# A decoder layer with a mixture of experts: order of fetches, routing steps and sends where attention ends

## The chip, the core and the metric

The kernel runs on one core of a Trainium2 chip. The metric is the device time of one launch in microseconds. Before the change three runs took 1261.08 us (median), from 1258.22 to 1261.12.

The engines are named as in the profile: PE (TensorE, matrix products and transposes), PEld (its weight loads), DVE (VectorE), ACT (ScalarE), POOL (GpSimd) and SP (SyncE, here only an issuer of DMAs).

## What is computed

A pre-norm decoder layer on 32 sequences of 112 tokens and 256 channels, all in float32: windowed causal self-attention, cross-attention to 375 context rows with a relative bias, and a feed-forward part in which each token goes to the two best of eight experts. Cut to the feed-forward part, which the change touches most:

```
x = x + self_attention(layernorm(x))
x = x + cross_attention(layernorm(x), ctx, rel_bias)

xf = layernorm(x).reshape(3584, 256)
probs = softmax(xf @ router_w.T)                       # 8 experts
topv, topi = top_k(probs, 2)
probs = probs * mask(topi)
probs = probs / (probs.sum(-1) + 1e-9)
h = silu(xf @ gate_w[e] + gate_b[e]) * (xf @ up_w[e] + up_b[e])   # 512 wide, per expert e
y = sum_e probs[:, e] * (h_e @ down_w[e] + down_b[e])
x = x + y
```

## The kernel before

**Groups and slots.** The 32 sequences form eight groups `g` of four. Attention is a software pipeline of numbered slots: each slot holds one item of scores, softmax and average of some group, and a table (`steps`, `late`) says which other steps are issued in which slot. `base[g]` is the first cross-attention slot of group g; a group takes 16 slots, and `base[NG]` (NG = 8) is the first slot after the last scores. PE, DVE and ACT run their instructions exactly in the order in which the slots issue them (`manual_schedule`), and POOL is held to the order of issue too (`pool_order`), apart from pairs of DMAs that are marked loose. So where a step stands in the table is where it stands in each engine's queue.

**Routing a group** (`put_route`). After its last norm (`norm`, `scale`, `norm_t`), a group's tokens go through seven steps, one slot each: `choose` (logits to exp), `rank` (softmax, then all comparisons of the eight probabilities), `front` (ties), `gate` (which two experts), `weight_gates` (the two weights), `count` (positions behind the tokens counted so far, in `taken`) and `address` (row numbers). Nearly every step is a DVE instruction, then a POOL one, then a DVE one. Then `send` scatters the group's normed rows into a DRAM buffer `xslots` in which each expert has its region: eight indirect DMAs from POOL, two for each of the four sequences. `turn_gates` and `down_bias` add the gate-weighted down bias to the residual `x`, and SP writes it to the output.

**Experts.** 39 tiles of 256 or 128 rows are worked off in the list `order`. For tile k, POOL issues an indirect fetch of the expert's weights (`fetch_weights`, 128 x 3080 floats, 1.58 MB) and one or two of its rows out of `xslots` (`fetch_rows`, 128 x 265 floats each). PE transposes the rows (`turned_in`, DVE copies them to `xT`), multiplies by gate and up weights (`hidden`, four steps f of eight matmul instructions; ACT `sil`, DVE `hid`), then by the down weights (`down`); ACT scales `y` and POOL scatters it into the output with an add. Tiles run one behind: `down` of tile k-1 comes after `hidden` of tile k. The first ten tiles are planned once six groups are counted, the rest after the last group (`later_plan`).

**The seam.** Tile 0's `hidden` steps are placed in the last attention slots (`begin`, `go_on`); `experts()` starts in slot `base[NG] + 5`, fetches tile 2 at once and tile k+3 when tile k starts. At this place the last group (g = 7) still has its norm and its whole routing ahead, and group 6 its sends: both are interleaved with the first expert tiles. PSUM tiles of kind `pj` (two buffers) are used by averages, `ops`, `count`, `gtp`, `dbps` and `py`, those of kind `sc` (four buffers) by scores and `gu`, those of kind `tr` (two) by transposes.

Lines that the prediction steps through: `fetch_weights` L949, `fetch_rows` L962, `send` L725, `turned_in` L1004 and L1008, `hidden` L1018 to L1026, `down` L1037 to L1044, `attended` L597 and L602, `divide` and `turn` L568 to L584, `count` L698 to L706, `rank` L641 to L651, `weight_gates` L676 to L688, `turn_gates` L749, `down_bias` L762 and L767, the last norm's POOL part L349 to L352 and its ACT part L363.

Of the kernel before, what the change touches and what calls it, by code (L numbers as in the profile page):

```python
# [11 lines left out]
F32 = mybir.dt.float32  # L12
# [7 lines left out]
B, S, D = 32, 112, 256  # L20
H, DH = 16, 16
K = 375
# [3 lines left out]
P = 128  # L26
GB = 4
NG = B // GB
# [50 lines left out]
def decoder_kernel(  # L79
# [95 lines left out]
    with ExitStack() as att, ExitStack() as own_att:  # L175
# [179 lines left out]
        def scale(g, n, b2):  # L355
            if b2 == 0:
                tag, width = ("xr", ROW) if n == 3 else ("xn", D)
                pool = keep if n == 3 else selfp
                xn = pool.tile([S, GB, width], F32, tag=tag, name=f"xn{g}_{n}")
                normed[g, n] = xn, *normed[g, n]  # L360
            xn, rstd, shift = normed[g, n]
            for b in (2 * b2, 2 * b2 + 1):
                nc.scalar.activation(  # L363
                    xn[:, b, :D], xs[g][:, b, :], AF.Identity,
                    bias=shift[:, b:b + 1], scale=rstd[:, b:b + 1],
                )
            if b2 == 1:
                normed[g, n] = [xn]
# [54 lines left out]
            )  # L423

        def cross_queries(g, c):
            if c == 0:
                cross_q[g] = two.tile([P, NC2, 2, GT], F32, tag="q_cross", name=f"q_cross{g}")
            ps = ps_pj.tile([P, GT], F32, tag="pj", name=f"q2ps{g}_{c}")
            project(ps, wq_sb[:, :, c * P:(c + 1) * P], normed[g, 2][1])
            by_parity(cross_q[g][:, c], ps, g == 0)  # L430

        def load_context(g, b):
            ct = two.tile([P, NC2, K], F32, tag="ct", name=f"ct{g}_{b}")
# [30 lines left out]
        def scores(cross, selfs):  # L464

            name = "_".join(str(v) for part in (cross or (), *selfs) for v in part)
            w = two.tile([S, 4, K + S], F32, tag="w", name=f"w{name}", bufs=3)
            low = small.tile([S, 3, 4], F32, tag="low", name=f"low{name}")
            at = K if cross else 0
            sc = [ps_sc.tile([S, 512], F32, tag="sc", name=f"sc{name}_{r}") for r in range(4)]  # L470
            if cross:
                g, b, s = cross
                c, p = divmod(s, 2)
                kT, q = keys[g, b][1], cross_q[g]
                for r in range(4):
                    rows = slice(32 * r, 32 * r + 32)
                    scored[cross] = nc.tensor.matmul(  # L477
                        sc[r][:, :K], q[rows, c, p, b * S:(b + 1) * S], kT[rows, c, :],
                        start=True, stop=True,
                    ).ins  # L480
            if selfs:
                g, b, s = selfs[0]
                c, p = divmod(s, 2)
                n, at_b = len(selfs), slice(b * S, (b + 1) * S)
                q, k = self_in[g, c]
                for r in range(4):
                    rows = slice(32 * r, 32 * r + 32)
                    nc.tensor.matmul(  # L488
                        sc[r][:, at:at + n * S].rearrange("q (p k) -> q p k", p=n),
                        q[rows, at_b], k[rows, p:p + n, at_b], start=True, stop=True,  # L490
                    )
            spans = []
            if cross:
                spans.append((0, K))
            spans += [(at + i * S, at + (i + 1) * S) for i in range(len(selfs))]
            for r in range(4):
                for i, (lo, hi) in enumerate(spans):
                    if cross and i == 0:
                        c, p = divmod(cross[2], 2)
                        add = bias[:, 8 * c + 2 * r + p, :]  # L500
                    else:
                        add = wmask
                    nc.vector.tensor_tensor_reduce(  # L503
                        out=w[:, r, lo:hi], in0=sc[r][:, lo:hi], in1=add,
                        scale=-1.0, scalar=FAR, op0=ALU.add, op1=ALU.min,
                        accum_out=low[:, i, r:r + 1],
                    )
            for i, (lo, hi) in enumerate(spans):
                nc.gpsimd.tensor_tensor(  # L509
                    w[:, :, lo:hi], w[:, :, lo:hi],  # L510
                    low[:, i].unsqueeze(2).to_broadcast([S, 4, hi - lo]), op=ALU.subtract,
                )
            return w
# [120 lines left out]
            nc.scalar.activation(pr, pr, AF.Exp)  # L634
            probs[g] = [pr]

        def rank(g):

            pr = probs[g][0]
            tot = small.tile([S, GB], F32, tag="tot", name=f"tot{g}")  # L640
            nc.vector.tensor_reduce(tot, pr, AX.X, ALU.add)  # L641
# [1 line left out]
            nc.gpsimd.tensor_tensor(  # L643
                pr, pr, tot.unsqueeze(2).to_broadcast([S, GB, E]), op=ALU.mult
            )
            mine = pr.unsqueeze(3).to_broadcast(four)
            other = pr.unsqueeze(2).to_broadcast(four)
            gt = small.tile(four, F32, tag="gt", name=f"gt{g}", bufs=1)
# [1 line left out]
            nc.vector.tensor_tensor(gt, other, mine, op=ALU.is_gt)  # L650
            nc.vector.tensor_tensor(eq, other, mine, op=ALU.is_equal)  # L651
            probs[g] += [gt, eq]

        def front(g):
            pr, gt, eq = probs[g]
# [14 lines left out]
            picked[g] = picks  # L670
            gates_of[g] = pr

        def weight_gates(g):
            pr = gates_of[g]
            tot2 = small.tile([S, GB], F32, tag="tot", name=f"tot2{g}")
            nc.vector.tensor_reduce(tot2, pr, AX.X, ALU.add)  # L676
            nc.gpsimd.tensor_scalar(tot2, tot2, 1e-9, None, op0=ALU.add)
            nc.vector.reciprocal(tot2, tot2)
            xn = normed[g, 3][0]
            gates = xn[:, :, D + 1:]  # L680
# [5 lines left out]
                gates.rearrange("s (b i) e -> s b i e", i=2),  # L686
            )
            nc.gpsimd.tensor_copy(xn[:, :, D], number[:, g * GB:(g + 1) * GB])  # L688
            gates_of.pop(g)

        rows_of = {}

# [13 lines left out]
                nc.vector.tensor_tensor(taken, taken, count[:, 1, cols], op=ALU.add)  # L706
            rows_of[g] = row

        def address(g):
            row, picks = rows_of[g], picked.pop(g)  # L710
            part = small.tile([S, 2, GB, E], F32, tag="part", name=f"part{g}")
            at = small.tile([S, 2, GB], F32, tag="at", name=f"at{g}")
            for k in range(2):
                nc.gpsimd.tensor_tensor(part[:, k], row, picks[:, k], op=ALU.mult)
            nc.gpsimd.tensor_tensor(part[:, 1], part[:, 1], part[:, 0], op=ALU.subtract)
            nc.vector.tensor_reduce(at, part, AX.X, ALU.add)
            to = small.tile([S, 2, GB], I32, tag="to", name=f"to{g}")
            nc.vector.tensor_copy(to, at)
            rows_of[g] = to

        def send(g, b):

# [219 lines left out]
        def fetch_weights(k):  # L942
# [6 lines left out]
            nc.gpsimd.indirect_dma_start(  # L949
                out=w, out_offset=None, in_=expert_w, in_offset=row_of(weigh_i[:, i:i + 1])  # L950
            )
            fetched[k] = [w]

        def fetch_rows(k):
            which, i, first, n = order[k]
# [5 lines left out]
            for h in range(n):  # L961
# [2 lines left out]
                    in_offset=row_of(rows_i[:, first + h:first + h + 1]),  # L964
                )
                follow(got.ins, all_sent[:2 * B * EARLY // NG] if which == 0 else all_sent, "rows")
            fetched[k].append(xg)

        def fetch(k):
            fetch_weights(k)  # L970
            fetch_rows(k)

        def target(k):

            which, i, first, n = order[k]
            aside, own = plans[which][2:4]
            xg, work = fetched[k][1], pool_of["work"]
            to = work.tile([P, 2], I32, tag="to", name=f"to{k}")
            gates = work.tile([P, 2, E], F32, tag="gates", name=f"gates{k}")
            gate = work.tile([P, 2], F32, tag="gate", name=f"gate{k}")  # L980
# [6 lines left out]
            nc.vector.tensor_reduce(gate[:, :n], gates[:, :n], AX.X, ALU.add)  # L987
            return to, gate

        def tiles_of(k):  # L990
            return pool_of["work" if k else "early"]

        def once(k, n=1):
            return {} if k else {"bufs": n}

        def hidden_of(k):
            return tiles_of(k).tile([P, NFC, 2 * P], F32, tag="hid", name=f"hid{k}", **once(k))

        def turned_in(k):
            n, xg = order[k][3], fetched[k][1]  # L1000
            tp = ps_tr.tile([P, NC2, 2 * P], F32, tag="tr", name=f"xtp{k}")
            for c in range(NC2):
                for h in range(n):
                    nc.tensor.transpose(  # L1004
                        tp[:, c, h * P:(h + 1) * P], xg[:, h, c * P:(c + 1) * P], ident
                    )
            xT = tiles_of(k).tile([P, NC2, 2 * P], F32, tag="xT", name=f"xT{k}", **once(k))
            nc.vector.tensor_copy(xT[:, :, :n * P], tp[:, :, :n * P])  # L1008
            return xT

        def hidden(k, xT, hid, f):
            st, w = order[k][3] * P, fetched[k][0]
            bias_at = 2 * NC2 * FF + NFC * D
            ps = ps_sc.tile([P, 2, 2 * P], F32, tag="sc", name=f"gu{k}_{f}")
            for m in range(2):
# [13 lines left out]
            )  # L1029

        def down(k, hid, to, gate):
            n, w = order[k][3], fetched.pop(k)[0]
            py = ps_pj.tile([P, 2, D], F32, tag="pj", name=f"py{k}")
            for h in range(n):
                for f in range(NFC):
# [20 lines left out]
            begun.extend((turned_in(0), hidden_of(0)))  # L1056

        def go_on(f):
            hidden(0, *begun, f)

        def experts():


            fetch(2)
            pending = None
            for k in range(len(order)):
                if k + 3 < len(order):
                    fetch(k + 3)
                if k:
                    hid = hidden_of(k)  # L1070
                    for f in range(NFC):
                        hidden(k, xT, hid, f)
                        if f == 1:
                            yield
                else:
                    hid = begun[1]
                    yield
                to, gate = target(k)
                yield
                if k + 1 < len(order):  # L1080
                    xT = turned_in(k + 1)
                if pending is not None:
                    down(*pending)
# [38 lines left out]
        def put_route(g, norm_at, norm_t_at):  # L1122
            put_norm(norm_at, norm_t_at, g, 3)
            put(norm_t_at + 1, logits, g)
            for i, fn in enumerate((choose, rank, front, gate, weight_gates, count, address)):
                put_late(norm_t_at + 1 + i, fn, g)
            for b in range(GB):
                put(norm_t_at + 8 + b, send, g, b)
            put(norm_t_at + 7, turn_gates, g)
            put(norm_t_at + 9, down_bias, g)  # L1130

# [78 lines left out]
        put(base[NG] + 2, go_on, 0)  # L1212
        steps[base[NG] + 3].insert(0, partial(go_on, 1))
        put(base[NG] + 3, go_on, 2)
        put_late(base[NG] + 4, go_on, 3)

        made = {}
# [107 lines left out]
```

## Time and profile before

| | |
|---|---|
| median of three runs | 1261.08 us |
| the profiled execution | 1270.69 us |
| its span, first to last instruction | 1269.0 us |
| PE busy | 1227.4 us, 97% of the span |
| POOL busy | 839.0 us, 66% |
| DVE busy | 651.0 us, 51% |
| ACT busy | 570.1 us, 45% |
| mean granted PE clock | 0.993 |
| chain that ended last | PE 92% of the span |

How to read it: PE is busy nearly all the time, and the chain of work that ended last runs through PE. The span has 41.6 us in which PE does nothing. The view of busy time by stretches shows where some of it lies (us of PE work in each 10 us, and the clock that was granted to it):

| stretch | PE busy | PE clock | DMA share |
|---|---|---|---|
| 870 to 880 | 9.49 | 1.00 | 0.01 |
| 880 to 890 | 7.43 | 1.00 | 0.00 |
| 890 to 900 | 7.06 | 0.79 | 0.22 |
| 900 to 910 | 8.47 | 0.87 | 0.25 |
| 910 to 920 | 8.35 | 1.00 | 0.60 |
| 920 to 930 | 4.87 | 0.66 | 0.81 |
| 930 to 940 | 10.00 | 1.00 | 0.40 |

The seam is this stretch. Ahead of it attention keeps PE at 9.5 us and more of every 10, behind it the experts do.

### The profile page before, as it was taken

To read this page: it belongs to the slowest core of one execution; us is meant where nothing else is said; L and a number is where in the kernel's file an instruction comes from. 1 tells how busy PE (TensorE), PEld (TensorE's weight loads), DVE (VectorE), ACT (ScalarE), POOL (GpSimd) and SP (SyncE) were. 2 spreads that over 40 slices of the span, in tenths; PEclk is the share of its full clock that TensorE was granted. 3 is DMA by queue.
4 is the path that set the end of the run, shared out by engine and by line. 5 is a ranking of instruction groups with operands and counts; after the bars stand their busy time and mean duration, and the time that the engine had idled before them with its cause. 6 is when DMAs were issued, how large, how long until landed. Compare 5 with 4: busy or idle time off the path is not lost.

```text
span 1269.0 us, 29648 instructions
## 1 busy us (share of the span) xinstructions
PE 1227.4 (97%) x11648; PEld 972.5 (77%) x11648; DVE 651.0 (51%) x3012; ACT 570.1 (45%) x1201; POOL 839.0 (66%) x784
## 2 busy tenths in 40 slices
PE   9999999999999999999999999998789999999997
PEld 6666776777787787778778777766678898888886
DVE  5653654665566566557566665665325323332221
ACT  4454554555556456555555545454222222222222
POOL 8545664577767777767776796687556655665552
PEclk9999999999999999999999999999889999999999
DMA  8129876731100200200110020130366778888882
GB/s 229 34 69 197 203 169 161 180 87 42 44 26 14 73 14 14 74 24 15 39 33 26 14 59 26 36 128 25 115 209 195 212 208 276 239 234 244 244 247 30
DMA packets 70204, 143.00 MB, mean 113 GB/s; under 512 B 5521, under 2 KB 60498, under 8 KB 65074
## 3 DMA queue, kind: packets, MB, share of 16 engines
q0 software_dynamic: 20784, 85.92, 23.1%
q1 hardware_dynamic: 49282, 55.20, 17.3%
q8 instruction: 92, 1.51, 0.5%
q14 instruction: 46, 0.38, 0.1%
HBM read 90.88 MB, written 50.21 MB: 111 GB/s over the span
## 4 chain that ended last, share of the span: by engine, by line
PE 92%; ACT 2%; DVE 2%; POOL 1%; issue 1%; another core or an unknown queue 1%; DMA 0%; POOLq 0%; ACTq 0%; DVEq 0%
PE gu L1018 18%; PE wT L530 14%; PE py L1037 9%; PE sc L477 8%; PE k2ps L383 6%; PE v2ps L450 6%; PE avc_s L554 6%; PE ops L597 4%; PE ctrwT L530 3%; PE sc L488 3%; PE vps L416 2%; PE qps L383 2%; PE q2ps L383 2%; PE kps L383 2%; PE tp L377 1%; ACT wT L531 1%
## 5 line engine op out<-in xcount | busy, mean ns | idle before, releaser
L509 POOL TENSOR_TENSOR w<-w,low 112x448 f32<-112x448 f32 (+1 forms) x256 | 459.4, 1814 | 211.1 <-DVE low L503 210.1
L503 DVE CUSTOM_DVE_ANT_0 w<-sc,bias 112x375 f32<-112x375 f32 x512 | 270.4, 542 | 118.2 <-PE sc L488 96.2
L531 ACT ACTIVATE wT<-wT 125x448 f32<-125x448 f32 (+1 forms) x394 | 199.0, 542 | 100.7 <-PE wT L530 94.3
L1018 PE MATMUL gu<-xT,w 128*128 128x256 f32 (+1 forms) x1248 | 229.9, 342 | 1.9 <-issue 1.9
L530 PEld LDWEIGHTS wT<-ident,w 112*125 112x125 f32 (+1 forms) x1576 | 187.6, 174 | 46.1 <-issue 14.2
L1018 PEld LDWEIGHTS gu<-xT,w 128*128 128x128 f32 x1248 | 202.1, 192 | 26.8 <-issue 5.7
L530 PE MATMUL wT<-ident,w 112*125 112x112 f32 (+1 forms) x1576 | 216.0, 275 | 5.8 <-ACT wT L531 5.8
L1026 DVE SCALAR_TENSOR_TENSOR hid<-gu,w,sil 128x256 f32<-128x256 f32 (+1 forms) x156 | 67.2, 432 | 233.6 <-ACT sil L1023 228.2
L1044 POOL DMA_INDIRECT out_dram<-y,to x63 | 100.4, 1594 | 111.8 <-ACT y L1043 94.2
L1023 ACT ACTIVATE sil<-gu,w 128x256 f32<-128x256 f32 (+1 forms) x156 | 67.5, 433 | 147.4 <-PE gu L1018 131.9
L503 DVE CUSTOM_DVE_ANT_0 w<-sc,wmask 112x112 f32<-112x112 f32 x512 | 129.0, 268 | 2.6 <-PE sc L488 2.6
L477 PE MATMUL sc<-kT,q_cross 32*112 32x375 f32 x1024 | 123.3, 518 | 1.3 <-DVE low L503 1.0
L1037 PE MATMUL py<-w,hid 128*128 128x256 f32 x504 | 116.8, 383 | 0.4 <-DVE x L767 0.4
L1037 PEld LDWEIGHTS py<-w,hid 128*128 128x128 f32 x504 | 94.0, 193 | 12.1 <-DVE x L767 0.6
L450 PE MATMUL v2ps<-wkv_sb,ct 128*125 128x256 f32 x384 | 94.3, 381 | 0.0
L383 PE MATMUL k2ps<-ct,wkv_sb 128*128 128x375 f32 x256 | 92.3, 483 | 0.0
L503 DVE DVE_READ_ACCUMULATOR2_ANT low<- 112x1 f32 x1024 | 84.0, 82 | 0.0
L602 DVE TENSOR_TENSOR x<-x,ops 112x256 f32<-112x256 f32 x64 | 24.8, 418 | 111.1 <-PE ops L597 110.9
L1043 ACT ACTIVATE y<-py,gate 128x256 f32<-128x256 f32 x63 | 27.2, 471 | 108.6 <-PE py L1037 106.8
L725 POOL DMA_INDIRECT xslots<-xn,to x64 | 61.8, 966 | 19.7 <-issue 14.8
L962 POOL DMA_INDIRECT xg<-xslots,rows_i x63 | 60.7, 963 | 18.9 <-issue 17.4
L450 PEld LDWEIGHTS v2ps<-wkv_sb,ct 128*125 128x125 f32 x384 | 67.2, 188 | 7.7 <-DVE q_cross L389 0.5
(208 smaller groups left out, 1646.6 us busy)
## 6 DMA issues: line engine op xcount, KB each, us to landing
xslots<-zeros SPq DMA_DIRECT2D x28, 1060.0 KB, 7.6
ct<-in_ctx_t_dram SPq DMA_DIRECT2D x32, 375.0 KB, 3.3
x<-in_x_dram SPq DMA_DIRECT2D x8, 448.0 KB, 6.6
out_dram<-x SPq DMA_DIRECT2D x8, 448.0 KB, 3.2
bias<-by_rel_d SPq DMA_DIRECT2D x1, 2625.0 KB
xslots<-xn,to POOLq DMA_INDIRECT x64
xg<-xslots,rows_i POOLq DMA_INDIRECT x63
out_dram<-y,to POOLq DMA_INDIRECT x63
```

Of the source, the lines that this page charges most:

```text
L383: nc.tensor.matmul(ps, w[:, k, :], xT[:, k, :], start=(k == 0), stop=(k == NC2 - 1))
L450: nc.tensor.matmul(ps[:, i, :], ct[:, k, j * KC:(j + 1) * KC], wkv_sb[:, k, D:2 * D], start=(k == 0), stop=(k == NC2 - 1),)
L477: scored[cross] = nc.tensor.matmul(sc[r][:, :K], q[rows, c, p, b * S:(b + 1) * S], kT[rows, c, :], start=True, stop=True,).ins
L503: nc.vector.tensor_tensor_reduce(out=w[:, r, lo:hi], in0=sc[r][:, lo:hi], in1=add, scale=-1.0, scalar=FAR, op0=ALU.add, op1=ALU.min, accum ...
L509: nc.gpsimd.tensor_tensor(w[:, :, lo:hi], w[:, :, lo:hi], low[:, i].unsqueeze(2).to_broadcast([S, 4, hi - lo]), op=ALU.subtract,)
L530: nc.tensor.transpose(tp[:m, r, :], w[:, r, lo:lo + m], ident[:S, :S])
L531: nc.scalar.activation(wT[:m, j], tp[:m], AF.Exp, scale=-1.0)
L554: nc.tensor.matmul(av[32 * r:32 * r + 32, i, p, :], v, x, start=(j == 0), stop=(j == n - 1),)
L1018: nc.tensor.matmul(ps[:, m, :st], w[:, lo:lo + P], xT[:, c, :st], start=(c == 0), stop=(c == NC2 - 1),)
L1023: nc.scalar.activation(sil[:, :st], ps[:, 0, :st], AF.Silu, bias=w[:, bias_at + f:bias_at + f + 1])
L1037: nc.tensor.matmul(py[:, h, :], hid[:, f, h * P:(h + 1) * P], w[:, lo:lo + D], start=(f == 0), stop=(f == NFC - 1),)
L1044: added = nc.gpsimd.indirect_dma_start(out=out, out_offset=row_of(to[:, h:h + 1]), in_=y[:, h, :], in_offset=None, compute_op=ALU.add,)
```

## The change

The edits, with the names of the table above:

1. **Cross-attention's queries** were one tile of both halves c in two buffers; now each half has a tile of its own in one buffer. The normed rows of a group that are sent (`xr`, n = 3) get two buffers in place of one.
2. **Fetches.** Rows are fetched in front of the weights of the same tile. `experts()` fetches tiles 2 and 3 at once; tile 4 comes at the start of tile 2 and tile 5 in its middle, tile 6 at tile 3, tile 7 at tile 4, from then on tile k+3 at tile k. Tile 1's transposes (`begin_next`) move in front of the last `attended` and of tile 0's last `hidden` step.
3. **The last group's routing.** `rank` is cut into `share` and `compare`, `weight_gates` into `total` and `spread_gates`, `address` into its POOL and its DVE part. For g = 7 the DVE part that waited for POOL stands in the next slot; the last step ends in the same slot as before, and its sends keep their slots.
4. **Group 6's sends** stand at slots 8, 10, 12, 14 behind its norm's transposes, instead of 8 to 11. For groups 6 and 7 `turn_gates` and `down_bias` come a slot later.

```diff
         def cross_queries(g, c):
-            if c == 0:
-                cross_q[g] = two.tile([P, NC2, 2, GT], F32, tag="q_cross", name=f"q_cross{g}")
+            cross_q[g, c] = one.tile([P, 2, GT], F32, tag=f"q_cross{c}", name=f"q_cross{g}_{c}")
...
+                xn = pool.tile(
+                    [S, GB, width], F32, tag=tag, name=f"xn{g}_{n}", bufs=2 if n == 3 else 1
+                )
...
         def fetch(k):
+            fetch_rows(k)
             fetch_weights(k)
-            fetch_rows(k)
...
+        def begin_next():
+            begun.append(turned_in(1))
...
             fetch(2)
-            pending = None
+            fetch(3)
+
+            ahead = {(2, 0): 4, (2, 1): 5, (3, 0): 6, (4, 0): 7}
+            ahead |= {(k, 0): k + 3 for k in range(5, len(order) - 3)}
+            pending, xT = None, begun[2]
             for k in range(len(order)):
-                if k + 3 < len(order):
-                    fetch(k + 3)
+                if (k, 0) in ahead:
+                    fetch(ahead[k, 0])
...
                         if f == 1:
                             yield
+                            if (k, 1) in ahead:
+                                fetch(ahead[k, 1])
...
-                if k + 1 < len(order):
+                if 0 < k < len(order) - 1:
                     xT = turned_in(k + 1)
...
-            for i, fn in enumerate((choose, rank, front, gate, weight_gates, count, address)):
-                put_late(norm_t_at + 1 + i, fn, g)
-            for b in range(GB):
-                put(norm_t_at + 8 + b, send, g, b)
-            put(norm_t_at + 7, turn_gates, g)
-            put(norm_t_at + 9, down_bias, g)
+            turn_at, bias_at, sends = 7, 9, range(8, 12)
+            route = [(fn,) for fn in (choose, rank, front, gate, weight_gates, count, address)]
+            if g >= NG - 2:
+                turn_at, bias_at = 8, 10
+            if g == NG - 2:
+                sends = 8, 10, 12, 14
+            if g == NG - 1:
+
+                route = (
+                    (choose,), (share,), (compare, front), (gate,), (total,),
+                    (spread_gates, count, address_parts), (whole_address,),
+                )
...
+        put(base[NG] + 4, begin_next)
         put_late(base[NG] + 4, go_on, 3)
```

Instruction counts of every engine stay the same. The order on DVE, PE and ACT differs in a few places, all in the last two groups' routing and around tiles 0, 1 and the group-7 steps; on POOL it differs from group 6's sends to the end, since rows now stand in front of weights there.

## The prediction
> **What bounds the kernel now.** I read the busy times first (PE 1227.4 of 1269.0 us), then the chain that ended last (PE 92%), then, for the 41.6 us without PE work, PE's row of the timeline with the gap ahead of each group. Behind 1000 us PE has no gap: a pair tile and a half tile repeat in 16.42 us to the hundredth. The edits can only be worth what lies at the seam. First its PE rows (start, length, line; in brackets the idle time ahead and who ended it):
>
> ```profile
> 886.71 0.35 PE L749 MATMUL gtp<-ident,gates_sb 112*64 112x112 f32 x2 [2.06 <-DVE taken L706]
> ...
> 895.70 2.04 PE L762 MATMUL dbps<-db_sb,gT 32*112 32x256 f32 x6 [2.62 <-ACT outs L558]
> 897.67 7.84 PE L1018 MATMUL gu<-xT,w 128*128 128x256 f32 x24
> 907.04 1.09 PE L597 MATMUL ops<-wo_sb,outs 128*112 128x256 f32 x4 [1.53 <-DVE outs L584]
> ...
> 911.94 3.69 PE L1018 MATMUL gu<-xT,w 128*128 128x256 f32 x16 [1.65 <-issue]
> ...
> 925.52 0.46 PE L626 MATMUL lg<-ident,lT 128*112 128x128 f32 x1 [5.13 <-ACT lT L620]
> ```
>
> Five gaps, 13.0 us. Two later ones are 0.30 (ahead of 942.95) and 0.40 (ahead of 974.50). Two of the five have no owner in the kernel, which the chain says:
>
> ```profile
> 890.76 4.52 another core or an unknown queue
> ...
> 921.27 3.92 another core or an unknown queue
> ```
>
> ACT waited there for PE, whose last matmuls end, as modelled, at 892.47 and 920.39, while the semaphore came only at 895.28 and 925.19. Elsewhere in this stretch it comes 14 ns behind the modelled end. No instruction of the program fills these 2.8 and 4.8 us. They also cost clock:
>
> ```profile
> 895.00:896.00 1.00, 0.30 (x2) 0.30 (x4) 0.00 (x0) 0.68 (x2) 0.00 (x0) 0.86 0.19 64
> 896.00:902.00 6.00, 6.00 (x16) 4.28 (x15) 1.38 (x3) 1.42 (x2) 0.00 (x0) 0.50 0.27 76
> 902.00:903.00 1.00, 1.00 (x5) 0.77 (x5) 1.00 (x2) 0.00 (x0) 0.00 (x0) 0.73 0.00 0
> ```
>
> In this view of busy time by stretches the third column from the right is the granted clock: half for 6.8 us (0.28 + 6 + 0.54). 24 matmuls took 7.84 us, at 0.216 each 5.2. With the slower `dbps` that is 2.9 us; behind the second wait (`py` 5.21 instead of 3.6, and transposes) 2.2 us.
>
> **Whose are these 12 us?** Waits 2.6 + 4.7 and clock 5.1 make 12.4. The profiled execution took 1270.69, 9.6 above the median, and the expert tiles, bound by PE, cannot stretch. So I take the unnamed waits for the profiler's own and leave them out of the sum. (The Trainium skill, "NOTIFIC — the notification-queue block", section 7.1, allows for it: its trace records can hold up an engine. No run here shows it.) What is left at the seam without them I rebuild by shifting the trace's own durations: gap 2.06 at `gtp`; about 1.45 at `ops`; 1.7 ahead of tile 1; 0.35 at `lg` (ACT's `lT` behind `sil`); about 0.9 for tile 2's rows; 0.7 later: 7.2 us. Everything below is against this rebuilt course, and stands for the median 1261.08.
>
> **Part by part.**
>
> *Queries and `xr`.* Half c = 1 is written in the slot of its last scores. ACT's write waits for the `q2ps` matmul, which stands behind those scores in PE's queue anyway: nothing. Without that cover it would be some 3 us a group. The second `xr` buffer is needed because ACT's L363 would otherwise wait for the later sends; before, the last had landed (910.57) when L363 started (911.77): nothing gained.
>
> *`turn_gates` of group 6 a slot later.* The 2.06 us are not its own: `count` and `gtp` share a `pj` buffer, and DVE read `count` late because
>
> ```profile
> 882.75 0.18 DVE L678 RECIPROCAL tot<-tot 112x4 f32<-112x4 f32 x1 [3.35 <-POOL tot L677]
> ```
>
> held DVE. That stays (only g = 7 is cut). Now `ops` takes that buffer and waits for the same event; one `ctrwT` group (0.44) runs ahead of it. Gain 0.5.
>
> *`down_bias` of group 6 behind `hidden` 1, tile 1's transposes ahead of `ops`.* `ops` waits for DVE's chain sil, hid, outs behind `hidden` 2 (0.48 + 0.48 + 0.36). Four transposes (0.43) now lie in it: 1.45 becomes about 1.05, gain 0.4. `xT` of tile 1 is copied ahead of the residual add: the 1.7 goes. What is late next: group 7's `tp`. PE reaches it 3.5 us after tile 1's start, but ACT's four L363 (2.08) need POOL's shift (N below), and DVE's norm has gained only about 0.3. Wait 0.9.
>
> *POOL: sends, rows, weights.* Let N be the end of the norm's POOL part (L352). Before, all eight sends are out by then and the weights follow at once:
>
> ```profile
> 908.01 0.94 POOL L725 DMA_INDIRECT xslots<-xn,to  x1 [0.30 <-issue]
> ...
> 911.49 0.25 POOL L352 TENSOR_SCALAR shift<-shift 112x4 f32<-112x4 f32 x1
> 912.23 1.10 POOL L949 DMA_INDIRECT w<-in_expert_w_dram,weigh  x1 [0.49 <-issue]
> 913.63 0.96 POOL L962 DMA_INDIRECT xg<-xslots,rows_i  x1 [0.30 <-issue]
> 914.89 0.95 POOL L962 DMA_INDIRECT xg<-xslots,rows_i  x1 [0.30 <-issue]
> ```
>
> By the trace's landing marks the weights landed at 919.5 (7.3 us after their issue), the second rows at 921.15 behind them. So before: weights N + 7.8, rows N + 9.4. After: two sends at N + 0.2 and 1.5 (1.25 each with the gap); the first rows then wait for the landing of the send just ahead of them, as the built program says (2.6 us from issue: 908.01 to 910.57), so start at N + 4.2 and 5.5, landing N + 8.3 (2.8 us, as tile 1's rows issued at 847.22 and landed at 850.0); weights at N + 6.7, landing N + 14.0. PE needs the rows at N + 7.1 (`tp` N + 2.6, two `hidden` 3.46, `lgps` 0.5, `lg` 0.6): wait 1.15 instead of 0.9. It needs the weights after `xtp` 0.43 and `py` 3.46, at N + 12.2: **a new wait of 1.8 us**. Queued behind on POOL: tile 3's rows and weights (N + 8 to 11.5), two sends that wait for those rows (N + 15), `y` of tile 0, then tile 4 (weights about N + 24, landing N + 31; PE is there at N + 35.6). These hide behind 10.8 us a tile.
>
> Two rules of the skill against this. "DMA: Bandwidth & Descriptors", Anatomy of one DMA, makes a POOL-issued transfer 2.0 us + bytes / 436 GB/s: 1.58 MB would land 5.6 us after issue, at N + 12.3, and the wait would be 0.1. The trace's row says 7.3, tile 0's weights (issued 839.97, landed 847.37) 7.4; I take 7.3. "TensorE: Matmul & The Clock Gate" (Why this matters for your kernels) asks for no idle gaps over about 3 us. Here idle of 3.0 and 5.1 us halved the clock, 2.06 did not. By the rule 1.15 and 1.8 cost themselves alone; but they lie 4 us apart, and if their sum counts, another 3.4 us (half of 6.8) is due. I take them alone and keep the other in the range.
>
> *Last group's routing.* DVE's
>
> ```profile
> 940.34 0.42 DVE L650 TENSOR_TENSOR gt<-pr 112x256 f32<-112x256 f32 x1 [3.65 <-POOL pr L643]
> ```
>
> goes behind `hid`; PE's 0.30 goes with it, and 0.40 at 974.50 with `down_bias` moved between `hidden` steps: 0.7. The final sends and `later_plan` keep their slots. SP's write of group 7 comes half a tile later, and POOL's next `y` scatter must wait for it: 448 KB take 3.2 us, PE doesn't wait for `y`; nothing.
>
> **The sum.** Gains 0.5 + 0.4 + 1.7 + 0.7 = 3.3; losses 0.9 + 0.25 + 1.8 = 2.95. Net -0.3; bounded by the weights' landing (wait from 0.1 to 3.5), the `tp` wait (0 to 1.5) and the clock (0 to 3.4): -3 to +5 for this case. Forecast **1260.5**, own range 1257.5 to 1265.
>
> **Cases.**
>
> - *A, even: 0.47.* As summed, 1260.5.
> - *B, the unnamed waits are in every run and the second goes: 0.20.* For it: both fall in POOL's bursts of DMA issues (889 to 894, 912 to 923), which the edit thins; the second lies under three weight fetches (DMA share 0.81), and after it `lgps` is over before the weights' packets start. Against: the 9.6 us and the undisturbed expert tiles, which fetch as densely. Gain 4.7 + 2.2, less the extra waits: 1254.5.
> - *C, slower through the late weights: 0.22.* Sends, a landing, then rows stand in front of tile 2's weights: 6.2 us later than before. For it: the wait in the built program. Against: `py` and `lgps` hide most. It decides from the point at which the weights land after N + 15 or the two gaps count as one: the half clock's 3.4 and a further 1 us: 1265.
> - *D, the weights are hidden: 0.11.* Landing by N + 12.2 as the skill's figure has it: the 1.8 goes, and `tp` doesn't wait: 1257.
>
> A measurement of this kernel tells about 0.3% (3.8 us) from no change. Faster by more: B nearly whole, D half, a little of A: 0.28. Slower: C mostly, a little of A: 0.24. Within: 0.48. The range over the cases: 1253 to 1265.5.
>
> **What would show it.** After: no gap ahead of tile 1's first `gu`; `ops` gap near 1; a gap at `tp` released by ACT L363; first L962 of tile 2 released by a send's landing; a gap ahead of tile 2's `gu` released by the weights' DMA; no 3.65 ahead of L650. I am wrong if the weights of tile 2 land before `py` ends, if half clock follows short gaps, or if the unnamed waits turn out not to be the profiler's.

## The result, and the profile after

The kernel after took **1266.96 us** (median of 9, 1264.80 to 1270.52) where the kernel before took 1261.08 (9 runs, 1258.22 to 1265.13): ratio **1.0051**, 95% interval 1.0037 to 1.0065. The forecast was 1260.5, with 1257.5 to 1265 as its range, up to 1265.5 over the cases. The change makes the kernel slower by half a per cent, and the interval lies clear of 1.

PE's rows of the timeline after, at the seam (start, length, line; in brackets the idle time ahead and who ended it):

```profile
889.07 1.12 PE L598 MATMUL ops<-wo_sb,outs 128*112 128x256 f32 x4 [1.02 <-DVE taken L721]
...
902.18 1.09 PE L598 MATMUL ops<-wo_sb,outs 128*112 128x256 f32 x4 [1.09 <-DVE outs L585]
903.11 5.34 PE L1043 MATMUL gu<-xT,w 128*128 128x256 f32 x24
...
914.37 0.32 PE L627 MATMUL lg<-ident,lT 128*112 128x128 f32 x1 [0.37 <-ACT lT L621]
916.64 0.33 PE L1027 MATMUL xtp<-ident,xg 128*128 128x128 f32 x1 [1.96 <-DMA xg<-xslots,rows_i]
917.81 0.90 PE L1027 MATMUL xtp<-ident,xg 128*128 128x128 f32 x3 [0.84 <-DMA xg<-xslots,rows_i]
918.51 6.26 PE L1062 MATMUL py<-w,hid 128*128 128x256 f32 x16
924.60 7.07 PE L1043 MATMUL gu<-xT,w 128*128 128x256 f32 x32
...
936.46 7.14 PE L1043 MATMUL gu<-xT,w 128*128 128x256 f32 x32 [0.89 <-ACT y L1068]
...
949.73 5.38 PE L1043 MATMUL gu<-xT,w 128*128 128x256 f32 x16 [2.24 <-issue]
```

The gap ahead of tile 1 is gone (the `gu` at 903.11 runs on from tile 0 into tile 1), and `ops` waits 1.09 as forecast. But there are two stalls that the sum had too small or not at all: 2.80 us at tile 2's transposes (1.15 in the sum), and 2.24 ahead of tile 4. Both bring half clock, as the view by stretches says (third column from the right):

```profile
917.00:923.00 6.00, 5.19 (x14) 4.25 (x15) 0.69 (x1) 0.00 (x0) 3.06 (x4) 0.50 0.88 314
...
951.00:955.00 4.00, 4.00 (x14) 3.16 (x12) 0.48 (x1) 0.47 (x1) 3.18 (x3) 0.57 0.96 271
```

That is why `py` took 6.26 us and not 3.6, and the first 16 `gu` of tile 4 took 5.38 and not 3.7. The clock records behind this view give whole windows of half clock, 3.4 or 6.8 us long: 6.8 from 917.0, 3.4 from 951.1. PE worked in 6.0 us of the first and in all of the second, so half clock cost 3.0 and 1.7 us.

**First stall.** POOL's rows of the same stretch:

```profile
908.67 0.95 POOL L748 DMA_INDIRECT xslots<-xn,to  x1 [0.30 <-issue]
913.72 1.01 POOL L985 DMA_INDIRECT xg<-xslots,rows_i  x1 [4.10 <-PE gu L1043]
915.03 0.95 POOL L985 DMA_INDIRECT xg<-xslots,rows_i  x1 [0.30 <-issue]
916.29 0.94 POOL L972 DMA_INDIRECT w<-in_expert_w_dram,weigh  x1 [0.30 <-issue]
...
924.77 0.96 POOL L748 DMA_INDIRECT xslots<-xn,to  x1 [3.79 <-DMA xg<-xslots,rows_i]
```

The releaser named for 913.72, PE, misleads: PE's signal is the last in a list of several. POOL's own wait records show a wait on the landing of the send at 908.67 that ended at 912.99; fifteen of that send's sixteen landing marks lie at 910.9 to 911.2, the last at 912.96. So the send took 4.29 us to land, POOL stood still, and tile 2's rows went out 6.6 us behind N, the end of the norm's POOL part. Then the next two sends waited 3.79 us for tile 3's rows.

What made one part late can be read from the DMA packets' times. The closing packets of fifteen parts (4 bytes each) were through at 910.87; the sixteenth started at 911.92, as a packet of 16 KB of the instruction queue (910.69 to 911.93) ended. The trace names no DMA engine, and no run moved that packet, so this is a reading and not a test. It is the same wherever this send stands at this place: in nine profiles (after, e2, e5, e6, e9, e10, e14, e16, e17) it landed after 3.89 to 4.47 us, each time with such a packet across it. In before and e18 the last send ahead of the fetches met none and took 2.56 and 2.59.

**Second stall.** Ahead of tile 4, all engines in order of time:

```profile
946.91 0.94 POOL L972 DMA_INDIRECT w<-in_expert_w_dram,weigh  x1 [0.30 <-issue]
...
947.88 0.35 POOL L675 TENSOR_SCALAR picks<-rank 112x32 f32<-112x32 f32 x1
948.17 0.31 POOL L676 TENSOR_SCALAR picks<-rank 112x32 f32<-112x32 f32 x1
948.56 0.25 POOL L677 TENSOR_TENSOR pr<-pr,picks 112x32 f32<-112x32 f32 x1
948.85 0.19 DVE L684 TENSOR_REDUCE tot<-pr 112x4 f32<-112x32 f32 x1 [3.86 <-POOL pr L677]
948.95 0.68 DVE L1033 COPY xT<-xtp 128x512 f32<-128x512 f32 x1
```

POOL issues fetches (the one at 946.91 is tile 6's weights) up to the moment at which it comes to the last group's `gate`. DVE's `tot` waits 3.86 us for it, the copy of tile 4's `xT` stands behind `tot`, and PE waits for `xT`. Tile 4's own weights had landed at 940.87. "issue" in PE's row is this: the releaser lay one engine further back.

### The profile page after: what moved, and what is told of

It is laid out like the page before. It is cut to its first block, busy times and chain, and to the rows that moved or that the text cites. A ratio compares the mean times of both kernels' runs of the same rounds, so it can differ in the third digit from the quotient of the medians.

```text
span 1266.3 us, 29617 instructions
## 1 busy us (share of the span) xinstructions
PE 1230.0 (97%) x11648; PEld 974.0 (77%) x11648; DVE 650.8 (51%) x3012; ACT 570.2 (45%) x1201; POOL 839.2 (66%) x784
## 4 chain that ended last, share of the span: by engine, by line
PE 90%; DVE 3%; POOL 2%; ACT 2%; issue 1%; DMA 1%; POOLq 0%; ACTq 0%; DVEq 0%
PE gu L1043 17%; PE wT L531 14%; PE py L1062 9%; PE sc L478 8%; PE avc_s L555 6%; PE k2ps L385 6%; PE v2ps L451 6%; PE ops L598 4%; PE sc L489 3%; PE vps L418 2%; PE qps L385 2%; PE ctrwT L531 2%; PE q2ps L385 2%; PE kps L385 2%; PE tp L379 1%; POOL w L510 1%
```

## The experiments

**Two kinds of sessions.** The runs were made in five sessions, each beside its own runs of the kernel before. In three of them before took 1257.9 to 1265.5 us, as in the first measurement; in two it took 1270.4 to 1279.2, and there every profile of before has the two unnamed waits. The chip that the record numbers 12 gave both kinds. So ratios are compared only within a kind. As a second measure I use the **seam**: from the `lg` of group 6 (about 865 us) to the end of the profiled span. It leaves out half-clock windows in attention, which come and go from one execution to the next (at 50, 92, 819 and 832 us). In the table, "sends 8 to 11" is after with group 6's sends where they were before the change, and "calm POOL" is after with the fetches of tile 5 and of some later tiles put off; the edits stand below.

| run | us | before | ratio, 95% | seam |
|---|---|---|---|---|
| *sessions without the unnamed waits* | | | | |
| before (e18) | 1262.91 | 1261.19 | 1.0009, 0.9999 to 1.0020 | 393.5 |
| after (first profile) | 1266.96 | 1261.08 | 1.0051, 1.0037 to 1.0065 | 401.5 |
| after (e5) | 1266.09 | 1261.83 | 1.0041, 1.0028 to 1.0054 | 402.2 |
| after (e17) | 1266.77 | 1261.19 | 1.0045, 1.0031 to 1.0059 | 399.5 |
| weights first (e6) | 1265.60 | 1261.83 | 1.0033, 1.0021 to 1.0044 | 398.3 |
| PE moves only (e7) | 1261.10 | 1261.83 | 0.9987, 0.9974 to 1.0000 | 394.3 |
| PE moves and routing cut (e12) | 1260.84 | 1261.20 | 0.9995, 0.9981 to 1.0008 | 394.1 |
| before, sends spread (e8) | 1281.53 | 1261.83 | 1.0145, 1.0121 to 1.0168 | 413.0 |
| no wait on sends (e9) | 1259.04 | 1261.20 | 0.9989, 0.9977 to 1.0001 | 392.1 |
| no wait, calm POOL (e10) | 1258.88 | 1261.20 | 0.9986, 0.9975 to 0.9998 | 392.0 |
| sends 8 to 11, calm POOL (e11) | 1259.22 | 1261.20 | 0.9978, 0.9967 to 0.9989 | 391.4 |
| *sessions with them* | | | | |
| before (e1) | 1273.44 | 1273.56 | 1.0006, 0.9991 to 1.0022 | 406.4 |
| before (e13) | 1273.80 | 1275.00 | 0.9995, 0.9985 to 1.0005 | 407.4 |
| calm POOL (e2) | 1267.06 | 1273.56 | 0.9945, 0.9925 to 0.9965 | 398.3 |
| calm POOL (e14) | 1267.42 | 1275.00 | 0.9945, 0.9927 to 0.9963 | 399.0 |
| sends 8 to 11 (e3) | 1266.03 | 1273.56 | 0.9939, 0.9918 to 0.9961 | 397.2 |
| sends 8 to 11 (e15) | 1265.31 | 1275.00 | 0.9932, 0.9913 to 0.9951 | 396.7 |
| sends 8 to 11, calm POOL (e4) | 1265.72 | 1273.56 | 0.9942, 0.9920 to 0.9963 | 396.1 |
| no routing cut (e16) | 1269.53 | 1275.00 | 0.9959, 0.9944 to 0.9974 | 400.1 |

### The base: before without and with the unnamed waits

> The kernel before, once more, with a second profile. Theory one (the unnamed waits of 2.6 and 4.7 us and the half clock behind them belonged to that one profiled execution): the new profile has no gap over 2.1 us between group 7's first norm step and tile 3, its seam is 7 to 9 us of idle, the profiled execution lies within 3 us of the others. Rival (they are in every run): the same two gaps at dbps and at lg, with half clock behind each, and a span about 1269 again. Time: 1261 by both, since nothing is changed.

> The kernel before. Theory: where its executions take 1258 to 1265, no gap ahead of dbps and 0.4 at lg; idle from gtp to tile 3's first gu 7 to 7.5 us, as rebuilt in the prediction. Rival (the base was mis-sized): idle under 6 or over 9 us.

> The kernel before, for its profile. Theory: on a chip where it takes 1261, no gap ahead of dbps, 0.4 at lg, idle from gtp to tile 3 of 7 to 7.5 us. On one where it takes 1273, the gaps of 2.6 and 5.0 again. Rival (the base was mis-sized): idle under 6 or over 9 us without the unnamed waits.

e1 and e13 fell in the sessions with the waits and missed what I expected of them: the waits did not belong to one execution. PE's rows of e13:

```profile
900.62 2.04 PE L762 MATMUL dbps<-db_sb,gT 32*112 32x256 f32 x6 [2.58 <-ACT outs L558]
...
930.12 0.46 PE L626 MATMUL lg<-ident,lT 128*112 128x128 f32 x1 [5.01 <-ACT lT L620]
```

e18 fell in one without, and is the profile that the prediction had to do without:

```profile
891.67 0.35 PE L749 MATMUL gtp<-ident,gates_sb 112*64 112x112 f32 x2 [2.06 <-DVE taken L706]
...
905.34 1.09 PE L597 MATMUL ops<-wo_sb,outs 128*112 128x256 f32 x4 [1.53 <-DVE outs L584]
...
910.24 3.69 PE L1018 MATMUL gu<-xT,w 128*128 128x256 f32 x16 [1.65 <-issue]
...
919.06 0.32 PE L626 MATMUL lg<-ident,lT 128*112 128x128 f32 x1 [0.37 <-ACT lT L620]
919.27 0.91 PE L1004 MATMUL xtp<-ident,xg 128*128 128x128 f32 x4
```

No gap at `dbps`, 0.37 at `lg`, no half clock at the seam. The idle sum with the two later gaps (0.30 and 0.40) is 6.3 us, not the rebuilt 7.2: the 0.9 that I put at tile 2's rows is not there. The seam is 13 us shorter than in e1 and e13, the rebuilt 12.4 nearly whole. What makes the waits is not settled. One thing goes with the sessions in all twenty profiles: in those with the waits (and in the profile of before that the prediction read) the trace holds 1777 to 1795 of PE's signals, and fewer of DVE's and ACT's too; in the others it holds 1840 of PE's.

### After, twice more

> The kernel after, once more, beside the same runs of before. Theory (whether the unnamed waits fall in an execution decides the sign: without them before spans about 1256.5 and after is 6 us slower, with them before spans 1269 or more and after, which shows none, is faster): where before's spans here are 1269 and more, after's are 1263 to 1267, ratio 0.994 to 0.998. Rival (the change costs 6 us whatever before does): ratio 1.004 to 1.006 again. Its profile should repeat the gap at xtp of tile 2 (2.8 us) and ahead of tile 4's gu (2.2 us).

> The kernel after. Theory (the change takes the unnamed waits out of PE's way and adds two stalls of its own): beside a before of 1273, 0.994 to 0.997 of it, 4 to 8 us faster; beside a before of 1261, 1.004 again. Rival (it costs the same on every chip): 1.004 in both.

Both fell in sessions without the waits: slower by 0.41 and 0.45%. The two stalls repeat in both (1.59 + 0.92 and 2.24; 2.02 + 0.88 and 2.23), and so does the landing (4.09 and 4.35 us). e5 has another window of half clock, which the first profile lacks, 3.4 us from 886.0, behind the same 1.02 us ahead of `ops`:

```profile
885.91 1.98 PE L598 MATMUL ops<-wo_sb,outs 128*112 128x256 f32 x4 [1.02 <-DVE taken L721]
```

Whether the change is a gain in a session with the waits was not measured for after itself. Its nearest relatives there are all under before (0.9959 and less); none of them has a gap ahead of `dbps`, where `hidden` steps now stand behind the average.

### The first stall: is it the wait for the sends?

Three edits, each to the kernel after. e9 declares what the data says: the first plan's rows come from groups 0 to 5, group 6's sends write others. e3 and e15 put the sends back; e6 turns only the order within a fetch.

```diff
e9
                 if which == 0:
+                    tc.declare_no_dep(got.ins, group="sent", reason="rows counted before")
+                    tc.add_to_no_dep_group("early_rows", got.ins)
...
+                if g >= EARLY:
+                    tc.declare_no_dep(sent.ins, group="early_rows", reason="rows counted later")
e3, e15
-                sends = 8, 10, 12, 14
+                sends = 8, 9, 10, 11
e6
-            fetch_rows(k)
             fetch_weights(k)
+            fetch_rows(k)
```

> After, with only this changed: the first plan's row fetches (their rows come from the six groups counted before) no longer wait for the landing of group 6's sends, nor those sends for the fetches. Theory two stalls (that wait makes tile 2's rows 5 us late): rows issued within 1 us behind the second send, gap at xtp under 0.5 us and no half clock behind it, 4 to 5 us faster than after where before has no unnamed waits, so level with before; POOL is earlier, so the gap ahead of tile 4 shrinks too. Rival (PE's reads of that memory hold the fetch): the fetch still starts near the end of tile 1's hidden steps, no gain.

> After, with group 6's sends in slots 8, 9, 10, 11 as before the change. Theory two stalls (tile 2's rows come late because two sends stand right in front of them and the rows wait for the last one's landing; PE idle 2.8 us, then 2.7 us of half clock): rows issued at once behind the norm, no gap at xtp, 1261.5; if POOL's queue drains earlier too and tile 4's stall goes with it, 1257. Rival (the rows are late for another reason, PE's reads of the memory they go to): gap at xtp stays over 2 us, 1266 to 1267.

> After, with group 6's sends in slots 8 to 11 and the fetches as in after. Theory: the gap at xtp goes (under 0.3 us) and with it 2.5 us of wait and 1.7 to 3.4 of half clock; POOL is some 7 us earlier, so the gap ahead of tile 4 shrinks to under 1 us too: 6 to 7 us faster than after, 0.998 to 0.999 of before. Rival (two separate costs): the gap ahead of tile 4 stays over 1.5 us, ratio 1.001 or more.

> After, with the weights of each tile fetched in front of its rows again. Theory two stalls (the rows wait for a send's landing whichever stands first, and POOL is as full as before): weights issued before the landing, rows no earlier than in after, the gap at xtp stays 2 to 4 us and the gap ahead of tile 4 stays 2 us, time within 2 us of after. Rival (the order of rows and weights is what costs): both gaps shrink below 1 us, 4 us or more faster than after.

POOL and then PE in e9:

```profile
909.02 0.95 POOL L748 DMA_INDIRECT xslots<-xn,to  x1 [0.30 <-issue]
910.27 1.01 POOL L987 DMA_INDIRECT xg<-xslots,rows_i  x1 [0.30 <-PE tp L379]
...
912.85 0.95 POOL L974 DMA_INDIRECT w<-in_expert_w_dram,weigh  x1 [0.30 <-issue]
...
917.85 0.97 POOL L748 DMA_INDIRECT xslots<-xn,to  x1 [0.30 <-issue]
```

```profile
914.71 0.32 PE L627 MATMUL lg<-ident,lT 128*112 128x128 f32 x1 [0.37 <-ACT lT L621]
914.87 0.60 PE L1032 MATMUL xtp<-ident,xg 128*128 128x128 f32 x4
915.31 3.62 PE L1067 MATMUL py<-w,hid 128*128 128x256 f32 x16
920.33 7.14 PE L1048 MATMUL gu<-xT,w 128*128 128x256 f32 x32 [1.40 <-DMA w<-in_expert_w_dram,weigh]
...
942.71 2.61 PE L1048 MATMUL gu<-xT,w 128*128 128x256 f32 x11 [0.54 <-ACT y L1073]
```

The rows go out right behind the send, although that send landed as late as in after (4.07 us). The gap at `xtp` is gone, no half-clock window follows, and the seam is 9.4 us shorter than in the first profile of after, against 4 to 5 expected: what went are 2.80 us of wait and 3.0 of clock at tile 2, and with POOL earlier also 0.89 ahead of tile 3 and 1.70 with 1.7 of clock ahead of tile 4; less a new 1.40 this makes 8.7. What is late next is named in the last two rows: 1.40 for tile 2's weights, the wait that the prediction had (1.8). PE's reads are ruled out as the cause.

e3 and e15, in sessions with the waits, have no gap at `xtp` either. PE comes there some 2.4 us later than in after, since the unnamed wait at `lg` is back (2.78 and 2.71), so these two alone would not show it; e11 below has the same sends, 0.37 at `lg` and no gap. The gap ahead of tile 4 stays in e3 and e15 in good part (1.66 and 1.61). So the second stall is no echo of the first: the rival of e15 was right on the gap, and its ratio fell beside a before with the waits. In e9 the gap is 0.54; that PE comes 1.40 us later there fits, but was not tested alone.

In e6 the first rows still wait for the landing, and here the profile names it:

```profile
912.29 0.95 POOL L985 DMA_INDIRECT xg<-xslots,rows_i  x1 [2.10 <-DMA xslots<-xn,to]
```

The gap at `xtp` is 2.83, the gap ahead of tile 4 is 2.24; the interval overlaps that of after. Which of rows and weights goes first is worth nothing that can be told here.

### The second stall: POOL's load, or the routing cut?

```diff
e2, e14
-            ahead = {(2, 0): 4, (2, 1): 5, (3, 0): 6, (4, 0): 7}
-            ahead |= {(k, 0): k + 3 for k in range(5, len(order) - 3)}
+            ahead = {(2, 0): 4, (3, 0): 5, (4, 0): 6, (5, 0): 7, (6, 0): 8, (6, 1): 9}
+            ahead |= {(k, 0): k + 3 for k in range(7, len(order) - 3)}
e16
-                route = (
-                    (choose,), (share,), (compare, front), (gate,), (total,),
-                    (spread_gates, count, address_parts), (whole_address,),
-                )
+                pass
```

> After, with tile 5 fetched at tile 3's start and not in the middle of tile 2, tile 6 at tile 4, tile 7 at tile 5, caught up at tile 6. Theory two stalls (PE waits 2.24 us ahead of tile 4 because POOL's queue is full of fetches and the routing step in it holds up DVE, which holds xT; half clock follows, 3.4 us): both go, 1261.3. Rival (POOL's load is not what holds it, the routing cut is): the gap ahead of tile 4 stays at 2 us or more, 1266 to 1267.

> After, with tile 5 fetched a tile later, sends and waits as in after. Theory (tile 4's stall is POOL's load on top of the late rows): the gap ahead of tile 4 goes, the gap at xtp stays at 2.5 us; 3 to 4 us faster than after (1266.1 beside a before of 1261.8), so 1.000 to 1.002 of before. Rival (echo: POOL's lateness from the rows alone makes it): gap ahead of tile 4 stays over 1.5 us, ratio 1.004.

> After, with the last group's routing steps whole as before the change. Theory (the cut has no share in the stalls): gaps at xtp and ahead of tile 4 as in after, time within 1.5 us of after, so 1.003 to 1.006 of before. Rival (the cut makes tile 4's stall, since its steps come a slot later on DVE): that gap goes, 3 to 4 us faster than after.

PE's rows of e14:

```profile
921.05 0.33 PE L1027 MATMUL xtp<-ident,xg 128*128 128x128 f32 x1 [2.11 <-DMA xg<-xslots,rows_i]
922.29 0.55 PE L1027 MATMUL xtp<-ident,xg 128*128 128x128 f32 x3 [0.91 <-DMA xg<-xslots,rows_i]
...
940.69 7.14 PE L1043 MATMUL gu<-xT,w 128*128 128x256 f32 x32 [1.64 <-ACT y L1068]
...
963.65 3.69 PE L1043 MATMUL gu<-xT,w 128*128 128x256 f32 x16 [0.69 <-ACT y L1068]
```

The gap ahead of tile 4 is gone (963.65 is tile 5), the first stall stays; e2 shows the same. So the gap ahead of tile 4 comes from POOL's load. Ahead of tile 3 there are 1.64 here. Both edits together take both stalls away (below). The ratio of e14 fell beside a before with the waits, so its forecast of 1.000 to 1.002 was not put to the test.

e16 missed what both sides expected. The stall didn't stay ahead of tile 4, nor go; it came a tile earlier and longer. DVE and PE:

```profile
936.85 0.43 DVE L654 TENSOR_TENSOR gt<-pr 112x256 f32<-112x256 f32 x1 [6.19 <-POOL pr L643]
```

```profile
939.46 8.83 PE L1043 MATMUL gu<-xT,w 128*128 128x256 f32 x32 [2.84 <-issue]
```

DVE's comparisons wait 6.19 us for POOL's `pr`, tile 3's `xT` behind them. In after, with the cut, DVE waits 1.93 us at the same step (its `gt` at 934.99), and that is the 0.89 ahead of tile 3. So the cut shortens this wait; with POOL as full as this, DVE then stands at a later step that needs POOL. What the cut is worth in time e16 doesn't say, since after was not run in its session.

### The parts on PE, and the sends alone

e7 is after with the fetches, group 6's sends and the last group's routing as before; e12 is e7 with the routing cut; e8 is before with one line changed.

```diff
e8
-                put(norm_t_at + 8 + b, send, g, b)
+                put(norm_t_at + 8 + (2 * b if g == NG - 2 else b), send, g, b)
```

> Before with only the steps moved on PE, DVE and ACT (queries, down_bias and turn_gates a slot later, tile 1's transposes early); fetches, sends and routing steps as before the change. Theory: the prediction's gains of 2.6 us at gtp, ops and tile 1 come, and the first unnamed wait has another group of gu behind it and costs PE nothing (2.6 us, and 3.4 us of half clock with it): 8 us under a before that has the waits, 2.6 under one that has not. Rival (another wait comes in its place): less than 2 us under before.

> Before with the steps moved on PE, DVE and ACT and the last group's routing cut; fetches and sends as before the change. Theory: 0.3 to 1 us faster than the same without the routing cut (1261.1 beside a before of 1261.8), so about 0.998 of before. Rival (the cut itself brings the stall ahead of tile 4): a gap of 1 us or more ahead of gu of tile 4 or 5, and slower than before.

> Before with only group 6's sends spread to slots 8, 10, 12, 14. Theory burst (PE's signal to ACT comes late only while POOL issues several sends or fetches in a row; the traces of after and of the calm variant, with spread sends, show no such delay at 892): the wait ahead of dbps and the half clock behind it go, the second one at lg stays or moves with the fetches; 3 to 6 us less idle there, against up to 6 us more from tile 2's late rows. Rival (the waits have nothing to do with the sends): the gap of 2.6 ahead of dbps stays.

e7's gains come (1.02 ahead of `ops`, 1.09, tile 1 without a gap; 3.1 us against e18), but PE is then at tile 2 sooner than its rows:

```profile
920.28 0.90 PE L1027 MATMUL xtp<-ident,xg 128*128 128x128 f32 x4 [1.67 <-DMA xg<-xslots,rows_i]
921.02 5.31 PE L1062 MATMUL py<-w,hid 128*128 128x256 f32 x16
```

1.67 of wait, a window of 3.4 us of half clock behind it (1.7), 0.34 at `tp`: 3.7, more than the gain, and its seam is 0.8 longer than e18's. Over its 14 runs 0.13% is left (interval 0 to 0.26%), so its rival was right. e12 misses its 0.998: the routing cut alone shows no gain.

e8 lay in a session without the waits, so it tells nothing of their cause. It shows another thing:

```profile
930.70 2.67 PE L377 MATMUL tp<-ident,xn 112*128 112x112 f32 x8 [16.80 <-ACT xn L363]
```

ACT waited 21.4 us for late sends to read the only `xr` buffer. That is the price of spread sends without the second buffer, which the change adds for this reason.

### Both stalls removed

e4 and e11 are after with the sends in slots 8 to 11 and the calm fetches; e10 has e9's edit and the calm fetches.

> After, with both edits: tile 5 fetched a tile later and group 6's sends in slots 8 to 11. Theory two stalls: what is left of the change are its gains on PE, no half clock at the seam, 1255 to 1257, faster than both kernels. Rival (only one of the two stalls is real, or they share a cause): no better than the better of the two single edits.

> After, with that wait removed and tile 5 fetched a tile later. Theory two stalls: neither gap, no half clock at the seam; 2 to 4 us under before where before has no unnamed waits, 8 or more under it where it has. Rival (a third cost of the change is left): not under before.

> After, with tile 5 fetched a tile later and group 6's sends in slots 8 to 11, once more in this company. Theory two stalls: within 1.5 us of the variant with the wait removed and the calm fetches, since both take away the same two stalls. Rival (the sends in a row delay PE's signals): slower than that one by 2 us or more, with an unnamed gap at lg.

PE's rows of e11:

```profile
918.40 0.32 PE L627 MATMUL lg<-ident,lT 128*112 128x128 f32 x1 [0.37 <-ACT lT L621]
918.56 0.60 PE L1027 MATMUL xtp<-ident,xg 128*128 128x128 f32 x4
...
922.46 7.07 PE L1043 MATMUL gu<-xT,w 128*128 128x256 f32 x32
...
944.05 3.62 PE L1043 MATMUL gu<-xT,w 128*128 128x256 f32 x16
...
956.15 3.69 PE L1043 MATMUL gu<-xT,w 128*128 128x256 f32 x16 [0.70 <-ACT y L1068]
```

It has no gap between `lg` and the end of tile 4 and no half clock at the seam; its gaps are 1.04 and 1.09 ahead of the two `ops`, 0.34 at `tp`, 0.37 at `lg` and 0.70 ahead of tile 5. It is 0.22% under before, interval 0.11 to 0.33%, the lowest ratio here (the intervals of e9 and e10 overlap it), and 0.6 to 0.7% under after by the ratios. e10 is within 0.4 us of it, as expected, short of the "2 to 4 us under before" by a little (1.8), with 1.30 of wait for tile 2's weights. In e4 the second unnamed wait is there (2.75 at `lg`), so the two ways differ there as its session has it.

## Why the prediction was wrong

- *What bounds the kernel; the unnamed waits left out of the sum*: right for the times shown, in which before took 1258 to 1265, while the profile of before (1270.69) is of the other kind. The reason given, the profiler's own in that execution, does not hold as put: whole sessions have them. The lost signal records speak for the recording as their source; no run shows it. The rebuilt seam was 0.9 us too long.
- *Gains on PE* (forecast 0.5, 0.4, 1.7): 1.04, 0.44, 1.65 in after. Right, the first too small; the sum left out that PE has one more gap of 0.26 and 0.3 us more work on the way.
- *`tp` waits 0.9 for ACT*: 0.34. Right in kind.
- *The second `xr` buffer is needed*: right; e8, without it, waits 21.4 us at ACT.
- **The step that failed**: "the first rows then wait for the landing of the send just ahead of them", taken as "2.6 us from issue", with "wait 1.15 instead of 0.9". The mechanism was right and its size was off. The landing took 4.29, POOL started again 0.76 behind it, and the rows went out at N + 6.6 instead of N + 4.2. The wait was 2.80, and before has none there (e18), so this term cost 2.80 and not 0.25. The landing time was taken from rows in which nothing crossed the send; what counts is the last of its sixteen parts.
- *"I take them alone"* (the clock at no cost): wrong. 0.37 and 1.96 us of idle were followed by 3.0 us of loss here, 1.7 in e5. With the window at tile 4 it was 4.7, beyond the bound of 3.4 that the sum named. "Half clock follows short gaps" was one of its own signs of being wrong.
- *A new wait of 1.8 for tile 2's weights*: not in after, since rows and clock came ahead of it: they landed 7.32 us after issue, as taken (7.3), at N + 16.5, and PE was there a microsecond later. With the first stall gone it shows, 1.40 in e9.
- **The step that was missing**: "These hide behind 10.8 us a tile" followed POOL's queue only as far as data: tile 4's weights hid indeed (landed 8.9 us early). The last group's POOL steps stand in the same queue, DVE in order behind them, and `xT` in order behind DVE. 2.24 us and 1.7 of clock.
- *Routing gain 0.7*: the 0.40 came; in place of the 0.30 ahead of tile 3 there are 0.89, since POOL's `pr` for the comparisons stands behind tile 4's fetch (issued at 933.74).

Against e18, PE in the first profile of after is 2.2 us sooner at `lg`, and gains 0.40 later. Against it stand waits of 2.80 + 0.59 + 2.24 = 5.6 and clock of 4.7. That makes 7.7 us, where its seam is 7.9 longer; e17, without the window at tile 4, is 6.0 longer. Case C had the sign and nearly the time (1265), but by luck: it named the weights, and it was the rows and a queue.

## What to carry to other kernels

An in-order engine that issues DMAs and also computes has one queue for both: for each fetch put in it earlier, ask which small computation now stands behind it, which engine waits in order for that, and what stands behind that wait. A tracked dependence on a whole buffer (rows written, rows read) turns "send, then fetch" into a stop for the landing; where the rows are known to differ, say so to the scheduler, or let the fetch not follow directly on a send. And a time saved on PE is only worth as much as the next transfer is early: e7 gave it all back at tile 2's rows.

## What the runs showed of the hardware

- A scatter of 112 rows with a 16 KB packet of the instruction queue across it landed after 3.89 to 4.47 us at one place of nine profiles; one that met none took 2.59 (e18). It depends on when the packet comes: the send at 891.63 in after, with one at 892.50 to 893.56, took 3.15. Other transfers go with late landings too: the send at 900.02 in after, beside SP's write of 448 KB, took 4.03.
- At the seam half clock came in windows of 3.4 or 6.8 us while PE worked on, and lasted 17.1 us in e8, where PE stood for 16.8. One gap's length does not tell whether it comes: the 1.02 to 1.04 us ahead of `ops` were followed by a window in e5 and e14, and by none in the thirteen other profiles that have this gap. In the same way 1.67 us were followed by one in e7 and 1.40 by none in e9, 2.08 by one in e13 and 2.06 by none in e18. "TensorE: Matmul & The Clock Gate" of the Trainium skill (Why this matters for your kernels) asks to keep idle gaps under about 3 us; in e5, e7 and e14 shorter ones were followed by half clock. The length of the windows agrees with the 3.4 us that the same page gives for the span the gate watches (Part 1).
- The same binary took 12 us more in some sessions than in others, on a chip with the same number, with two waits that no instruction explains. A profile and times of different sessions can disagree by more than a change is worth.
